# A graph network on 16 graphs: the next graph's sums and inverses move one layer earlier

## The chip, the cores and the metric

The kernel runs on one core of one Trainium2 chip. A core has a matrix engine (TensorE, PE in the profile, with its weight loads shown apart as PEld), three engines for vectors (VectorE or DVE, ScalarE or ACT, GpSimd or POOL) and SyncE (SP), which here issues nearly all DMA transfers. Each engine works through its own queue in order and waits on semaphores for the others. The metric is the device time of one execution in microseconds. The time before is 2472.18 us, the median of three runs (2469.78 to 2474.06).

## The reference

The inputs are `x`, 16 graphs of 1024 nodes with 128 features, and `adj`, a 1024 x 1024 matrix of weights for each graph, all in fp32.

```
# part 0
degree = adj.sum(axis=-1)[:, :, None]
nbr    = einsum('bid,bij->bjd', x, adj) / degree
x      = layernorm(x + relu(concat([x, nbr], -1) @ W.T + b))
# part 1: four layers on the same adj
src = nodes @ ws + bs;   src_agg = einsum('bjv,bij->biv', src, l2norm(adj, axis=2))
dst = nodes @ wd + bd;   dst_agg = einsum('bjv,bji->biv', dst, l2norm(adj, axis=1))
out = tanh(concat([src_agg, nodes @ wn + bn, dst_agg], 2) @ wu + bu)
```

The second and the later layers of part 1 get earlier outputs as well (inputs of 128, 128, 256 and 384 features). Its result gets a residual and a layer norm too. So each graph needs of its matrix: the sums of its rows (the degree), the sums of squares of its rows, and the sums of squares of its columns; the inverses of the first and the inverse roots of the others scale rows or columns.

## The kernel before

**Batches.** The kernel goes through the 16 graphs one after the other, here called batches 0 to 15. Its matrix `a` lies in SBUF as 128 partitions x 8 row blocks x 1024 columns. Two such buffers exist: while batch b is worked on, the matrix of batch b + 1 (`a2`, of index n in the code) is loaded, its sums are made, and part 0 of batch b + 1 is done. The first matrix has a start of its own.

**Layers.** Each layer l of part 1 first makes messages (`messages`, L605 and L608): the features times folded weights, in four groups of two row blocks, with half 1 of the nodes first (groups 2, 3, 0, 1); PE makes a group, DVE adds the bias. Then it aggregates (`aggregate`, L774) over the matrix scaled by columns (`a`) and over its transpose scaled by rows (`at`). The product is done by halves in the way of Strassen and Winograd, with seven products and sums of quarters of the matrices made by DVE: T2, T3, T4 from `a` and Q2, Q3, Q4 from `at` (`combine`, L587 to L591). Each step of the loop is a pair of matmuls on 64 columns of the array each, which run side by side. Layers zero and one have 30 steps, of which the first two are the layer's own weights; layer two has 32. M2 on Q2 begins at step 14 in layer one of batch 0, M3 on Q3 at step 18, Z21 on T4 at step 22 and on Q4 at step 26. Results of products are read between the steps: copies on ACT (L687, L688, L691, L692, L708), additions on DVE (L695, L712, L699, L703, L704) and at last L776; the tanh that ends each half is L787, and its output (f1T, f23T) is what the next layer's messages read.

**Hooks.** The order of the work on PE, DVE, ACT and POOL is written out by hand: what the program says first stands first in the queue of its engine. A dictionary of hooks gives, for a step of the aggregation, a function that is called ahead of that step's matmuls; `between` does so behind a group of the messages. A hook says only where its instructions stand in the queues. Its PE instructions do stand between two steps; DVE and ACT may come to theirs earlier or later. The order of DMA issues on SyncE is chosen by the framework.

**Sums of the next matrix.** ACT squares a row block (L253, with the row sum of squares as a by-product) into one of two buffers of tag `sq`, and sums a row block for the degree (`degree_of`, L248 on ACT, L246 on DVE). DVE adds the eight squares up, two buffers into `acc` first (L260) and then one after the other (L262). `column_sums` turns `acc` over in 32 x 32 pieces (L270) and reduces it to `part` (L275). `inverses` multiplies that by a constant (pc, L183 on PE), brings it to the right places (L299, L301, L306) and lets POOL raise all to the power -1/2 (L307). `inverse_rows` (L328 to L331) makes the inverse degree and writes all inverses to DRAM (`dr`, L333). `factor_row` reads a row of it back to all partitions (`cinv`, later `dinv`, L339). DVE scales the next matrix with `cinv` (L345, 16 instructions), then makes its quarters (L583, L452), the sums of x (`x_sums`, L441 to L445, on `xn` that `load_blocks` loads, L205), and `first_gnn` does part 0 of the next batch on PE: products at L516, sums T3 and T4 at L461 and L467, reads at L498 to L518, and last the weights (pw, L183), which read e1 (L508) and e0 (L518). It stands between layers two and three.

**Layer norm of the batch before.** In layer one its last norm is done: `begin1` (L354 to L361), `centre1` (pm on PE, L368, square L371 on ACT), `squares1` (L377), `rstd1` (pv on PE, L385, POOL L387); L392 and the stores of the output (L235) follow in layer two (`end1`).

**Buffers.** Tiles of one tag share a buffer, and the later one waits for the last reader of the earlier one. `acc` has tag "row", which `cinv` and `dinv` use as well; the intermediate sums of layer one have tag "acc".

Of the kernel before, what the change touches and what calls it, by code (L numbers as in the profile page):

```python
# [14 lines left out]
P = 128  # L15
# [8 lines left out]
def adj_resnorm_kernel(ctx: ExitStack, tc: tile.TileContext, x, adj, w0, b0, layers, out):  # L24
# [231 lines left out]
    def add_squares(b, state, i):  # L256

        if i == 1:
            state["acc"] = one.tile([P, N], F32, tag="row", name=f"acc{b}")
            nc.vector.tensor_add(state["acc"], state[0], state[1])  # L260
        elif i > 1:
            nc.vector.tensor_add(state["acc"], state["acc"], state[i])  # L262

    def column_sums(b, state):

        column_reduce(b, state, column_transpose(b, state))
# [69 lines left out]
    def factor_row(b, state, k, tag):  # L336
        r = one.tile([P, N], F32, tag="row", name=f"{tag}{b}")
        for h in range(NH):
            nc.sync.dma_start(r[:, half(h)].rearrange("p (g i) -> p g i", g=G),  # L339
                              state["dv"][k, h][None].to_broadcast([P, G, P]))  # L340
        return r
# [239 lines left out]
    def combine_1(y):  # L581

        nc.vector.tensor_sub(y[0, 1], y[0, 1], y[0, 0])  # L583

    def combine(i, y, T):
        if i == 2:
            nc.vector.tensor_sub(T[2], y[1, 1], y[0, 1])  # L587
        elif i == 3:
            nc.vector.tensor_sub(T[3], T[2], y[0, 0])
        else:  # L590
            nc.vector.tensor_sub(T[4], y[1, 0], T[2])  # L591
# [404 lines left out]
    for b in range(B):  # L996
# [8 lines left out]
        if b == 0:  # L1005
            def row_factors0():
                nonlocal rinv
                rinv = gather_inverses(0, row_inverses(0, inv))
                column_sums(0, st0)
                for q in (2, 3):  # L1010
                    scale_rows(rows[q], q, rinv)

            t = messages(b, 0, feats, wm, {0: lambda: to_x1(0), 2: row_factors0}, with_sums=False)
            cinv = {}

            def columns0(rows, h, engine=nc.vector):
                scale_columns(a, cinv[0], rows, half(h), engine)

            def rows0(destination, finish):
                for q in (2, 3):  # L1020
                    transpose_rows(rows[q], q, at)

            def cinv0(destination, finish):
                cinv[0] = factor_rows_now(0, 1, inv, "cinv")

            def second0(destination, finish):
                columns0(range(NJ, NB), 1)
                destination(1, cinv[0])
                columns0(range(NJ), 1)

            def fold_and_scale(l, q):
                fold_begin(l, fetched[l])
                scale_rows(rows[q], q, rinv)

            def first0(destination, finish):
                columns0(range(NJ, NB), 0, nc.gpsimd)
                columns0(range(2), 0, nc.gpsimd)
                for q in (0, 1):
                    transpose_rows(rows[q], q, at)
                destination(0, cinv[0])  # L1040
                columns0(range(2, NJ), 0)

            def sums0(destination, finish):
                combine_1(y)
                finish(1)
                combine(2, y, T)
                combine_1(yt)
                combine(3, y, T)

            def folded(l, part):  # L1050
                return lambda *_: part(l, fetched[l])

            hooks = {4: lambda *_: inverses(0, st0, NB), 5: folded(2, fold_begin), 6: rows0, 7: cinv0,
                     8: folded(2, fold_end), 9: lambda *_: fold_and_scale(3, 0), 11: second0, 12: folded(3, fold_end),
                     14: lambda *_: scale_rows(rows[1], 1, rinv), 18: first0, 26: sums0}
            T = combined(0, "T")
            plain_layer(b, 0, feats, t, a, at, f1, "acc", hooks)
            wm = message_weights(b, 1)
            a2 = load(n)
            xs2 = load_spread(n)  # L1060
        else:
            w = {}
            if nxt:
                w["a"] = load(n)
                st = begin_sums(n)
            t = messages(b, 0, feats, wm)
            wm = message_weights(b, 1)
            Q = combined(b, "Q")

            def rows3():  # L1070
                for q in (1, 0):
                    transpose_rows(rows[q], q, at)

            def sums1(w=w, st=st):
                if nxt:
                    for i in range(2):
                        squares_of_row(n, w["a"], st, i)
                    for i in range(2):
                        degree_of(w["a"], st, i)

            hooks = {0: rows3, 3: lambda: combine(4, y, T), 5: lambda: combine_1(yt), 7: lambda: combine(2, yt, Q),
                     9: lambda: combine(3, yt, Q), 11: lambda: combine(4, yt, Q),
                     17: sums1}
            aggregate(b, 0, feats, t, a, at, T, Q, f1, "row", hooks)
            a2, xs2 = w.get("a"), None

# [6 lines left out]
        def sums_of(*rows, of=(), engine=nc.scalar, add=()):  # L1093

            def issue():
                for i in of:
                    degree_of(a2, st, i, engine)
                for i in rows:
                    squares_of_row(n, a2, st, i)
                for i in add:  # L1100
                    add_squares(n, st, i)
            return issue

        hooks = {}
        if b == 0:
            def quarters2():
                for i in (2, 3, 4):
                    combine(i, yt, Q)

            hooks = {0: quarters2, 12: lambda: combine(4, y, T)}  # L1110
            st = begin_sums(n)
            hooks |= {5 + 2 * i if i < 3 else 4 + 3 * i: sums_of(i, of=(i,), engine=nc.scalar if i < BPH else nc.vector, add=(i,))
                      for i in ALL}
        else:
            nm = f"1_{b - 1}"
            w = {"ys": summed(f"y{nm}", "xa")}
            sums_of_next = {}
            if nxt:
                sums_of_next = {1: sums_of(2, 3, of=(2, 3), add=(2, 3)), 4: sums_of(of=(4, 5)), 10: sums_of(4, 5),
                                13: sums_of(add=(4, 5)), 16: sums_of(6), 17: sums_of(7),  # L1120
                                19: sums_of(of=(6,), add=(6,)), 22: sums_of(of=(7,), add=(7,)),
                                23: lambda: column_sums(n, st)}

            def begin1(w=w, nm=nm):
                if nxt:
                    add_squares(n, st, 1)
                norm_spread(w["ys"], f4, KS)
                w["s"] = norm_sum(w["ys"], KS, nm, back)

            def centre1(w=w, nm=nm):  # L1130
                w["sq"] = norm_centre(w["ys"], w["s"], KS, nm)
                if nxt:
                    w["xs"] = load_spread(n)

            def squares1(w=w, nm=nm):
                w["v"] = norm_squares(w["sq"], KS, nm)

            def rstd1(w=w, nm=nm):
                w["r"] = norm_rstd(w["v"], KS, nm)

            hooks = {0: begin1, 12: centre1, 14: squares1, 20: rstd1, **sums_of_next}
        aggregate(b, 1, feats, t, a, at, T, Q, f23, "acc", hooks)
        if b:
            second_norm, xs2 = w, w.get("xs")

# [11 lines left out]
        def start3(w=w):  # L1157
            w["xT"] = to_features(xs2, f"x{n}_")

        def sums3():  # L1160
            column_sums(n, st)

        def factors(w=w):
            w["xn"] = load_blocks(n)
            inverse_rows(n, st)
            w["cinv"] = factor_row(n, st, 1, "cinv")

        def factors_of_rows(w=w):
            w["spread"] = row_inverses(n, st["inv"])
# [18 lines left out]
        if nxt:  # L1188
            scales = [lambda: scale(0, 1), lambda: scale(NJ, 1), lambda: scale(0, 0), lambda: scale(NJ, 0)]
            if b == 0:  # L1190
                between = {1: sums3}
                hooks = {4: inverses3, 5: factors, 10: factors_of_rows, 11: start3, 18: factors_gathered,
                         **dict(zip((12, 15, 19, 25), scales))}
                quarters_at = (26, 27, 29)
            else:
                between = {0: inverses3, 1: end1, 2: factors}
                hooks = {0: factors_of_rows, 3: start3, **dict(zip((7, 9, 11, 13), scales)), 15: factors_gathered}
                quarters_at = (19, 21, 25)
            hooks |= dict(zip(quarters_at, (quarter1, x_sums, quarter2)))
        t = messages(b, 2, feats, wm, between)  # L1200
        wm = message_weights(b, 3)
# [154 lines left out]
```

## Time and profile before

| | |
|---|---|
| time | 2472.18 us (2469.78 to 2474.06) |
| span of the profiled execution, clock | 2471.2 us, 0.998 |
| busy: PE, DVE, ACT, POOL | 2444.3, 1913.8, 954.4, 273.6 us |
| batch 7: layer zero, messages, layer one, messages, layer two | 25.90, 3.65, 26.13, 7.54, 27.64 us |
| batch 7: aggregation for the next batch (L516), pw (L183) | 12.02, 4.00 us |
| batch 0: layer one, messages, layer two, then L516 and pw | 25.90, 12.99, 27.75, 22.01 us |

A line of the stretches reads: begin and end in us, length, then for PE, PEld, DVE, ACT and POOL the busy time with the number of instructions, the clock that TensorE was granted (1.00 is full), and the share and rate of the DMA engines. In a line of the timeline stand start, length, engine, line of the kernel, operation, what it writes and reads, shapes, and in brackets how long the engine was idle before it and what ended that. A line of the waits has who waited for whom, the total in us, how often, and the longest. The ends of matmuls are modelled, so PE counts as busy in most of its short waits; the distances between starts tell more.

### The profile page before, as it was taken

The numbers are of one execution on the slowest core, as the hardware profiler recorded it, in microseconds if no ns is written. First come the engines' busy times: TensorE is split into PE (matmuls) and PEld (weight loads), VectorE is DVE, ScalarE is ACT, GpSimd is POOL, SyncE is SP. The second block draws the span as 40 slices with busy tenths as digits, with TensorE's granted clock in tenths as the row PEclk, the third lists the DMA queues.
The fourth block names the chain that finished last, engine by engine and source line by source line (L and its number), as shares of the span: only waits on it lengthen the run. The fifth ranks groups of instructions, "written<-read, shape, count | busy, mean of one in ns | idle before, by whom it ended". The sixth has DMA issues, their size and how long they took to land. (4 is left out here: it accounts for less than half of the span.)

```text
span 2471.2 us, 30800 instructions
## 1 busy us (share of the span) xinstructions
PE 2444.3 (99%) x11453; PEld 1028.7 (42%) x11453; DVE 1913.8 (77%) x2499; ACT 954.4 (39%) x1786; POOL 273.6 (11%) x100
## 2 busy tenths in 40 slices
PE   8999999999999999999999999999999999999999
PEld 5443344433444334443444434334443344433444
DVE  5868878788787987778787787887878878798743
ACT  5315345153342534426243351534515334253321
POOL 4001111001111011110111100111101111101100
PEclk9999999999999999999999999999999999999999
DMA  9517244272542616335172452724426254261410
GB/s 206 101 40 151 58 96 94 59 141 52 115 90 62 132 43 137 75 78 108 44 162 51 89 103 54 145 58 94 95 60 141 52 116 92 58 132 43 95 24 9
DMA packets 365716, 219.68 MB, mean 89 GB/s; under 512 B 152768, under 2 KB 336832, under 8 KB 365568
## 3 DMA queue, kind: packets, MB, share of 16 engines
q1 hardware_dynamic: 364800, 215.36, 41.1%
q0 software_dynamic: 768, 2.36, 0.4%
q8 instruction: 91, 1.49, 0.3%
q14 instruction: 57, 0.47, 0.1%
HBM read 199.17 MB, written 18.46 MB: 88 GB/s over the span
## 5 line engine op out<-in xcount | busy, mean ns | idle before, releaser
L774 PE MATMUL m<-Q,S 128*64 128x512 f32 x1008 | 445.1, 593 | 1.3 <-DVE Q L587 1.3
L387 POOL TENSOR_TENSOR rs<-ve,mhalf 128x32 f32<-128x32 f32 x30 | 191.6, 6387 | 1975.1 <-DVE ve L385 1975.1
L774 PE MATMUL m<-T,S 128*64 128x512 f32 x1008 | 396.6, 593 | 0.0
L774 PE MATMUL m<-at,t 128*64 128x512 f32 x1008 | 394.4, 593 | 0.0
L774 PE MATMUL m<-a,t 128*64 128x512 f32 x1008 | 390.1, 593 | 0.0
L608 DVE TENSOR_TENSOR t<-pt,wm 128x512 f32<-128x512 f32 x256 | 176.5, 690 | 162.0 <-PE pt L605 160.0
L774 PEld LDWEIGHTS m<-Q,S 128*64 128x64 f32 x1008 | 136.2, 137 | 282.0 <-issue 269.8
L687 ACT COPY e<-m 64x512 f32<-64x512 f32 x63 | 36.7, 582 | 511.0 <-PE m L774 510.6
L774 PE MATMUL z<-a,S 128*64 128x512 f32 x504 | 228.3, 593 | 0.0
L774 PE MATMUL z<-a,t 128*64 128x512 f32 x504 | 226.8, 592 | 0.0
L774 PE MATMUL z<-at,S 128*64 128x512 f32 x504 | 226.7, 592 | 0.0
L774 PE MATMUL z<-at,t 128*64 128x512 f32 x504 | 226.6, 592 | 0.0
L774 PE MATMUL z<-Q,t 128*64 128x512 f32 x504 | 226.6, 592 | 0.0
L605 PE MATMUL pt<-wm,f1T 128*128 128x256 f32 x768 | 216.0, 387 | 0.1
L345 DVE TENSOR_TENSOR a<-a,cinv 128x512 f32<-128x512 f32 x250 | 154.3, 691 | 78.3 <-DMA cinv<-dr 77.0
L774 PEld LDWEIGHTS m<-at,t 128*64 128x64 f32 x1008 | 118.5, 137 | 143.9 <-issue 142.5
L774 PEld LDWEIGHTS m<-a,t 128*64 128x64 f32 x1008 | 120.1, 137 | 134.1 <-issue 121.3
L774 PE MATMUL z<-T,t 128*64 128x512 f32 x384 | 172.8, 592 | 0.0
L774 PEld LDWEIGHTS m<-T,S 128*64 128x64 f32 x1008 | 119.0, 137 | 127.3 <-issue 127.3
L605 PEld LDWEIGHTS pt<-wm,f1T 128*128 128x128 f32 x768 | 142.7, 190 | 44.4 <-issue 13.5
L605 PE MATMUL pt<-wm,f23T 128*128 128x256 f32 x512 | 153.4, 381 | 3.7 <-ACT f23T L787 3.7
L253 ACT ACTIVATE sq<-a 128x1024 f32<-128x1024 f32 x120 | 125.8, 1050 | 79.0 <-DVE acc L260 78.3
(239 smaller groups left out, 4281.4 us busy)
## 6 DMA issues: line engine op xcount, KB each, us to landing
a<-in_adj_dram SPq DMA_DIRECT2D x120, 512.0 KB, 11.0
a<-in_adj_dram SPq DMA_DIRECT2D x240, 128.0 KB, 4.2
rows<-in_adj_dram SPq DMA_DIRECT2D x240, 64.0 KB, 2.7
wm<-wsave SPq DMA_DIRECT2D x16, 512.0 KB, 4.1
xn<-in_x_dram SPq DMA_DIRECT2D x124, 64.0 KB, 1.9
wm<-wsave SPq DMA_DIRECT2D x31, 256.0 KB, 3.4
xs<-in_x_dram SPq DMA_DIRECT2D x60, 128.0 KB, 3.6
cinv<-dr SPq DMA_DIRECT2D x30, 256.0 KB, 5.5
```

The costliest lines, as they stand in the source:

```text
L253: nc.scalar.activation(sq, a[:, i, :], AF.Square, accum_out=state["cols"][:, i:i + 1])
L345: engine.tensor_mul(a[:, i, s], a[:, i, s], cinv[:, s])
L387: nc.gpsimd.tensor_tensor(rstd, ve, mhalf[:, :n], ALU.pow)
L605: nc.tensor.matmul(pt[:, q], f[:, i * P:(i + 1) * P], wm[:, 1 + c], start=(k == 0), stop=(k == nch - 1))
L608: nc.vector.tensor_add(t[j][:, o:o + 2].rearrange("p k a v c -> p k (a v c)"), pt, wm[:, 0][:, None, :].to_broadcast([P, 2, 2 * P]))
L687: nc.scalar.copy(e0[high], A[high])
L774: nc.tensor.matmul(o, x, y, start=start, stop=stop)
```

## The change

The change moves the sums of the next matrix, and what hangs on them, to earlier places. Its parts:

- In batches 1 to 15 the first addition of squares moves from layer one into layer zero (step 28). `acc` takes the tag "acc" and the sums of layer one take "row", so that `acc` can be written while layer zero still uses "row".
- In those batches the hooks of layer one are set anew, squares and row sums first, and `inverses` with its product pc moves from behind the second message group of layer two to step 29 of layer one. The norm's `centre1` and `rstd1` move one and two steps ahead.
- `factors` (inverses to DRAM and the row `cinv` back) follows the second message group, ahead of the norm's end and the loading of x, and the scaling of the matrix, its quarters and the sums of x take earlier hooks. The transpose of the next x (`start3`, L350) moves behind them.
- In batch 0 all row sums are done by ACT, the sums start with layer one and alternate with Q2, Q3, T4 and Q4, column sums move to step 27 of layer one, and `inverses` and `factors` into the messages of layer two.

```diff
@@ add_squares
-            state["acc"] = one.tile([P, N], F32, tag="row", name=f"acc{b}")
+            state["acc"] = one.tile([P, N], F32, tag="acc", name=f"acc{b}")
@@ layer zero, batches 1 to 15
+            def first_addition(st=st):
+                if nxt:
+                    add_squares(n, st, 1)
+
-                     17: sums1}
+                     ... 17: sums1, 28: first_addition}
@@ layer one, batch 0
-            def quarters2():
-                for i in (2, 3, 4):
-                    combine(i, yt, Q)
-
-            hooks = {0: quarters2, 12: lambda: combine(4, y, T)}
+            hooks = {0: sums_of(0, 1, add=(1,)), 1: lambda: combine(2, yt, Q), 2: sums_of(2, 3, add=(2, 3)),
+                     3: lambda: combine(3, yt, Q), 4: sums_of(4, 5, of=(0, 1), add=(4, 5)), 5: lambda: combine(4, y, T),
+                     11: sums_of(of=(2, 3)), 13: sums_of(6, 7, of=(4,)), 15: sums_of(of=(5,)),
+                     18: lambda: combine(4, yt, Q), 19: sums_of(of=(6, 7), add=(6, 7)), 27: lambda: column_sums(n, st)}
             st = begin_sums(n)
-            hooks |= {5 + 2 * i if i < 3 else 4 + 3 * i: sums_of(i, of=(i,), engine=nc.scalar if i < BPH else nc.vector, add=(i,))
-                      for i in ALL}
@@ layer one, batches 1 to 15
-                sums_of_next = {1: sums_of(2, 3, of=(2, 3), add=(2, 3)), 4: sums_of(of=(4, 5)), 10: sums_of(4, 5),
-                                13: sums_of(add=(4, 5)), 16: sums_of(6), 17: sums_of(7),
-                                19: sums_of(of=(6,), add=(6,)), 22: sums_of(of=(7,), add=(7,)),
-                                23: lambda: column_sums(n, st)}
+                sums_of_next = {1: sums_of(2, 3, add=(2,)), 2: sums_of(of=(2, 3, 4, 5)), 8: sums_of(4), 10: sums_of(add=(3,)),
+                                12: sums_of(5, add=(4,)), 15: sums_of(6, add=(5,)), 19: sums_of(7, add=(6,)),
+                                20: sums_of(of=(6,)), 21: sums_of(add=(7,)), 23: sums_of(of=(7,)),
+                                24: lambda: column_sums(n, st), 29: lambda: inverses(n, st)}
             def begin1(w=w, nm=nm):
-                if nxt:
-                    add_squares(n, st, 1)
-            hooks = {0: begin1, 12: centre1, 14: squares1, 20: rstd1, **sums_of_next}
-        aggregate(b, 1, feats, t, a, at, T, Q, f23, "acc", hooks)
+            hooks = {0: begin1, 11: centre1, 14: squares1, 18: rstd1, **sums_of_next}
+        aggregate(b, 1, feats, t, a, at, T, Q, f23, "row", hooks)
@@ layer two
-        def sums3():
-            column_sums(n, st)
-
         def factors(w=w):
-            w["xn"] = load_blocks(n)
             inverse_rows(n, st)
             w["cinv"] = factor_row(n, st, 1, "cinv")
+
+        def load_xn(w=w):
+            w["xn"] = load_blocks(n)
+
+        def end1_and_load():
+            load_xn()
+            end1()
             if b == 0:
-                between = {1: sums3}
-                hooks = {4: inverses3, 5: factors, 10: factors_of_rows, 11: start3, 18: factors_gathered,
-                         **dict(zip((12, 15, 19, 25), scales))}
-                quarters_at = (26, 27, 29)
+                between = {1: inverses3, 3: factors}
+                hooks = {1: load_xn, 5: factors_of_rows, 7: start3, 18: factors_gathered,
+                         **dict(zip((10, 12, 14, 16), scales))}
+                quarters_at = (20, 22, 25)
             else:
-                between = {0: inverses3, 1: end1, 2: factors}
-                hooks = {0: factors_of_rows, 3: start3, **dict(zip((7, 9, 11, 13), scales)), 15: factors_gathered}
-                quarters_at = (19, 21, 25)
+                between = {0: factors, 1: end1_and_load}
+                hooks = {2: factors_of_rows, **dict(zip((4, 5, 7, 9), scales)), 10: factors_gathered, 16: start3}
+                quarters_at = (12, 14, 25)
```

In the diff, `sums_of(rows, of=, add=)` squares the row blocks `rows`, sums those of `of` for the degree and adds the squares of `add`; `quarters_at` gives the hooks of the first quarter, the sums of x and the second quarter.

More of the change, by code (lines that the diff above doesn't have):

```diff
@@ L1079, in sums1 @@
                         degree_of(w["a"], st, i)
+            def first_addition(st=st):
+                if nxt:
+                    add_squares(n, st, 1)
             hooks = {0: rows3, 3: lambda: combine(4, y, T), 5: lambda: combine_1(yt), 7: lambda: combine(2, yt, Q),
-                     9: lambda: combine(3, yt, Q), 11: lambda: combine(4, yt, Q),
-                     17: sums1}
+                     9: lambda: combine(3, yt, Q), 11: lambda: combine(4, yt, Q), 17: sums1, 28: first_addition}
             aggregate(b, 0, feats, t, a, at, T, Q, f1, "row", hooks)
```

## The prediction

> **What bounds the kernel now.** I read the page first, then who TensorE (PE) waited for, then stretches of the trace by stage, then the queues of VectorE (DVE), ScalarE (ACT), GpSimd (POOL) and the DMA issuer SyncE around each gap. The page says that PE has work for 99% of the span, so time can come only out of PE's own gaps.
>
> ```profile
> PE 2444.3 (99%) x11453; PEld 1028.7 (42%) x11453; DVE 1913.8 (77%) x2499; ACT 954.4 (39%) x1786; POOL 273.6 (11%) x100
> ```
>
> The waits of PE between 84 and 176 us, batch 0's layers one and two, name the only two long gaps after the start:
>
> ```profile
> PE m_f L516 <- DVE xn L443: 3.7, 1, 3.7
> PE pt L605 <- ACT f23T L787: 3.7, 2, 2.2
> ```
>
> Four stretches of batch 0 (layer one; messages of layer two; layer two; the aggregation for batch 1, L516 and L183) beside the last batch's messages, where nothing is late:
>
> ```profile
> 84.86:110.76 25.90, 25.90 (x121) 8.55 (x121) 22.82 (x21) 12.76 (x25) 0.00 (x0) 1.00 0.32 50
> 110.76:123.75 12.99, 9.33 (x35) 7.01 (x33) 10.63 (x12) 4.02 (x7) 0.00 (x0) 0.87 0.09 27
> 123.75:151.50 27.75, 27.75 (x137) 9.47 (x137) 17.57 (x34) 4.85 (x8) 2.90 (x1) 1.00 0.16 46
> 151.50:173.51 22.01, 18.28 (x74) 6.69 (x71) 18.75 (x29) 5.54 (x9) 0.00 (x0) 0.92 0.09 25
> ...
> 2387.40:2394.50 7.10, 7.10 (x34) 5.99 (x32) 2.76 (x4) 0.72 (x1) 0.00 (x0) 1.00 0.00 0
> ```
>
> The messages take 12.99 us against 7.10: 5.9 us lost. The last stretch takes 22.01 us against 12.02 + 4.00 in batch 7: 6.0 us lost. In both the granted clock falls to 0.5 after the wait (the 0.87 and 0.92).
>
> Later batches lose little but often. After the aggregation for the next batch, PE multiplies its result by the weights (pw, L183) and waits for DVE:
>
> ```profile
> 1228.30 1.03 PE L183 MATMUL pw<-e_f,w0T 128*64 128x512 f32 x4
> 1229.58 1.08 PE L183 MATMUL pw<-e_f,w0T 128*64 128x512 f32 x4 [0.25 <-DVE e_f L518]
> ```
>
> and over the 14 pw stretches of batches 1 to 14 together (4.19 us each; the sum of the stretches first, then busy times):
>
> ```profile
> sum 58.72, PE 54.40 PEld 12.37 DVE 38.42 ACT 13.21 POOL 0.00; mean PE 3.89 PEld 0.88 DVE 2.74 ACT 0.94 POOL 0.00
> ```
>
> Matmuls start there 0.43 us apart when nothing waits, so eight starts and 0.1 us to the next stage need 3.53 us; 58.7 - 14 x 3.53 = 9.3 us are waits. In batch 7 DVE reaches that point late because its scaling of the next matrix started late:
>
> ```profile
> 1197.05 9.72 DVE L345 TENSOR_TENSOR a<-a,cinv 128x512 f32<-128x512 f32 x16 [4.97 <-DMA cinv<-dr]
> ...
> 1228.83 0.69 DVE L518 TENSOR_TENSOR e_f<-e_f,dinv 128x512 f32<-128x512 f32 x1
> ```
>
> [...] ACT stands 8.22 us before one square while row sums behind it are ready. [...] in batch 0 dr is issued at 131.94 and cinv at 133.42. [...]
>
> **The change, part by part.**
>
> *Column sums and inverses of the next matrix, batches 1 to 14.* The first addition moves into layer zero (step 28). DVE ends L704 there at 1148.48 and starts L776 at 1149.73, so 1.22 us fit in idle time: cost nothing. That frees both square buffers 8 us earlier, so ACT squares rows 2 and 3 at 1151 and not at 1158; all its sums still lie beside PE work.
>
> The product pc then stands in PE's queue ahead of step 29 of layer one and not behind the second message group. Times are from the layer's start, 1153.26. Steps are 0.8586 apart, two small products add 0.23, so step 29 comes at 25.2. DVE's chain to pc's operand: M2 ends at step 18, L695 can start at 15.85; with the starts that the trace has between such instructions L712 follows after 1.37, then 0.72, 0.22, 1.27, 1.14, 0.72, 0.79, 0.61 and 1.28 (L385, two additions, L699, L703, L704, L270, L275), and L275 takes 1.22. It ends at 25.2: PE waits about 0.1 us, or 0 to 0.4. ACT is not in the way (square of row 6 ends at 16.1, its copy L696 is wanted at 16.55). For this pc leaves a place where it costs 7.54 - 7.10 = 0.44 us (it splits a run of 256-column matmuls) for one where a like product, rp, shifts the row by 0.12. Per batch -0.44 + 0.12 + 0.12 = -0.20: **-2.8 us** over 14, with ends of -4.5 and +1.
>
> *Factor rows.* POOL's power (2.90 us) now starts at about 26.3, not 29.5, and DVE has invt at 30, 1183.3 in batch 7. dr no longer stands behind the four stores of the output (issued from 1185.44), so it goes at 1183.3 and not 1188.21; with batch 0's 1.5 us to cinv and 5.5 to the first scaling (133.42 to 138.89), and up to 1 us for the stores now beside it, scaling starts at 1191 to 1192, not 1197.05. The transpose of x (1.25 us) moves behind it. DVE then has everything before L695 done by 1204.9, when PE delivers, instead of 1209.10, and from there follows PE: L776 1214.8 (was 1217.54), L498 1221.75 (was 1223.06). Z0 is ready at 1226.85, so L517 and L518 end at 1228.35; PE wants that at 1229.1. The waits of pw go: **-9.3 us** of 14 batches, at worst -5 if some lateness stays.
>
> *Batch 0, layer one.* Row sums leave DVE (four of 1.2 us), and Q2, Q3 and T4 alternate with additions. DVE: addition 88.54, Q2 to 92.0 (wanted at step 14, 97), Q3 to 96.6 (100.4), T4 to 101.2 (103.9). ACT from 89.8, when the first addition frees the buffers: four squares and two row sums at 1.09 to 96.4, three copies to 98.2, three row sums and two squares to 103.6, two copies to 104.7, a row sum to 105.8, then L696. This is a new wait: L712 needs L696 and stands at the head of DVE from 101.9 to 106.5, with Q4 behind it; Q4 ends at 109.5 and PE wants it at step 26, 107.2. PE stops about 2.2 us (0.5 to 3) and ends the layer at 113.0, not 110.76. DVE goes on with two additions, L699, L703, L704 (to 114.0), tanh to 114.8: PE waits 1.4 us for f23T where it waited 1.47. The column sums end at 116.4, L776 at 117.0, tanh at 117.8, before PE wants it at 118.8, so the wait of 2.19 and the slow clock behind it go. pc costs 0.44 here. Layer two starts at 122.1 against 123.75: **-1.7 us**, between -4 (ACT quicker) and +1 (half clock after the new stop, 1.7 us, partly inside the next wait).
>
> *Batch 0, layer two.* inverses follows group two: POOL 119.6 to 122.5, dr at 123.5 beside the weights' DMA, cinv at about 126.5, scaling at 132 and not 138.89. Sixteen at 0.61 end at 141.8; quarter one, x's sums (1.7) and L695 to L704 bring DVE to 149.6 and quarter two to 152.6. The aggregation for batch 1 starts at 149.75 and wants T2 at 153.2, T3 at 156.6, T4 at 158.3; L461 ends at 155.7, L467 at 158.3. The wait of 3.73 us and the slow clock go: 17.67 becomes 12.02, **-5.7 us**, and pw loses another **-0.4**.
>
> Nothing else changes what PE waits for: the waits for Q2 in layer zero (L587, 2.6 us together) stay. Sum: -2.8 - 9.3 - 1.7 - 5.7 - 0.4 = -19.9, or 2452.3; I say **2453**.
>
> **Rivals.** *Only batch 0 gains:* the stores delay cinv, or L518 stays late for another cause, and pc's new wait eats what its place saves. For it: the pw waits vary from 0.2 to 1.3 us between like batches, which my chain doesn't explain. Against: all of DVE's lateness in batch 7 is accounted for. 2472.2 - 7.8 = 2464.4. *More than I sum:* ACT runs ahead in batch 0, Q4 comes in time, pc never waits: -1.7 more for pc and -2.3 more in layer one, 2448.5. *Slower:* pc now stands ahead of matmuls that are ready, so any lateness of the last addition is paid by PE. Were ACT one square and one row sum late (2.2 us) in all 14 batches, +31, less the 9.3 and 7.8 that stay: 2486. For it: no slack on DVE. Against: ACT has half a microsecond to spare, and its total work is unchanged.
>
> **How the numbers follow.** Forecast 0.67, only batch 0 0.13, more 0.14, slower 0.06 with smaller lateness in it. The range holds the forecast with its bounds and the better case, and reaches to the first rival without going far beyond: 2447 to 2464. Faster by over 0.2% (4.9 us) 0.94: the first three. Within 0.2% 0.03 and slower 0.03 share the last.
>
> **What would show it.** Right: in the stretches of batch 0 the messages of layer two near 9 us with one wait near 1.4 us on f23T; a wait of m or z on Q (L591) near 107 us in layer one; no wait on xn L443, clock 1.00 after 125 us; pw stretches near 3.5 us; messages of layer two at 7.1 us in batches 1 to 14 and layer one at 26.2 to 26.4; first scaling 5 us earlier. Wrong: pw waits unchanged, or PE waits on part L275 of over 0.4 us each.

## The result, and the profile after

The changed kernel takes 2456.17 us (2455.62 to 2456.82), the kernel before 2470.98 us beside it (2468.33 to 2474.06): a ratio of 0.994, 95% interval 0.9922 to 0.9957. It is faster by 14.8 us, where 19.2 were forecast; the predicted time of 2453.0 is 3.2 us short, and the measured one lies within the range. The profiled spans are 2471.2 and 2454.6 us, 16.6 apart: the execution of the kernel before that was profiled took 2472.99 us, 2.0 over the median.

The page after, PE's busy time, which was 2444.3:

```profile
PE 2433.6 (99%) x11453; PEld 1026.5 (42%) x11453; DVE 1909.8 (78%) x2495; ACT 956.8 (39%) x1794; POOL 287.2 (12%) x100
```

Whom PE waited for in batch 0's layers one and two (the same 84 to 176 us as before):

```profile
PE z L774 <- DVE Q L591: 1.9, 1, 1.9
PE pt L605 <- ACT f23T L787: 1.1, 1, 1.1
PE pw L183 <- DVE e_f L518: 0.3, 1, 0.3
```

The wait of 3.7 us on xn L443 is gone and the one on f23T is cut from 3.7 to 1.1; a new one on Q4 stands in layer one. The same four stretches as before (layer one; messages of layer two; layer two; L516 and L183):

```profile
84.69:112.67 27.98, 26.12 (x121) 8.46 (x120) 23.20 (x21) 19.00 (x37) 0.00 (x0) 1.00 0.26 42
112.67:121.58 8.91, 7.81 (x38) 6.03 (x37) 6.32 (x11) 1.57 (x3) 2.40 (x1) 1.00 0.21 57
121.58:149.21 27.63, 27.63 (x133) 9.36 (x134) 21.46 (x37) 3.97 (x7) 0.51 (x1) 1.00 0.21 58
149.21:165.55 16.34, 15.99 (x74) 4.88 (x70) 14.20 (x23) 6.42 (x11) 0.00 (x0) 1.00 0.00 1
```

Layer one costs 2.1 us more, its neighbour 4.1 less, the last stretch 5.7 less, and the clock is 1.00 in all four, where it was 0.87 and 0.92 in two.

The 14 pw stretches of batches 1 to 14, summed as before:

```profile
sum 49.42, PE 49.42 PEld 14.08 DVE 25.23 ACT 9.64 POOL 0.00; mean PE 3.53 PEld 1.01 DVE 1.80 ACT 0.69 POOL 0.00
```

They took 58.72; now each takes the 3.53 us of a stretch without a wait. Where the time went, as distances between the starts of the stages on PE (without the rounding of the stretches above):

| stage | before | after | difference |
|---|---|---|---|
| batch 0: layer one | 25.90 | 27.98 | +2.1 |
| batch 0: messages, layer two | 40.74 | 36.54 | -4.2 |
| batch 0: L516 | 17.67 | 12.02 | -5.65 |
| batch 0: pw | 4.35 | 4.32 | 0.0 |
| batches 1 to 14: layer zero | 365.17 | 365.27 | +0.1 |
| layer one | 365.88 | 372.49 | +6.6 |
| messages of layer two | 105.56 | 99.46 | -6.1 |
| layer two and L516 | 555.11 | 555.11 | 0.0 |
| pw | 58.72 | 49.47 | -9.3 |

The sum is -16.4, the whole difference of the spans but for 0.2, by which the start ahead of layer one was shorter. Two rows nearly cancel: what the messages gain by losing pc, layer one gives back.

### The profile page after: what moved, and what is told of

It reads as the page before. It is cut to its first block, busy times and chain, and to the rows that moved or that the text cites. A ratio compares the mean times of both kernels' runs of the same rounds, so it can differ in the third digit from the quotient of the medians.

```text
span 2454.6 us, 30806 instructions
## 1 busy us (share of the span) xinstructions
PE 2433.6 (99%) x11453; PEld 1026.5 (42%) x11453; DVE 1909.8 (78%) x2495; ACT 956.8 (39%) x1794; POOL 287.2 (12%) x100
## 4 chain that ended last, share of the span: by engine, by line
PE 84%; DVE 6%; DMA 5%; SPq 1%; ACT 1%; issue 1%; DVEq 0%; POOLq 0%; ACTq 0%
PE m L774 37%; PE z L774 21%; PE pt L605 15%; PE m_f L516 5%; DMA a<-in_adj_dram 3%; PE pw L183 2%; PE z_f L516 2%; SPq L549 1%; DVE at L564 1%; DMA rows<-in_adj_dram 1%; DVE acc L262 1%; DMA rows_acc<-in_adj_dram 1%; DMA raw<-in_L_gnn_ws_dram 1%; DVE at L583 1%; DVE Q L587 0%
## 5 line engine op out<-in xcount | busy, mean ns | idle before, releaser
L387 POOL TENSOR_TENSOR rs<-ve,mhalf 128x32 f32<-128x32 f32 x30 | 205.2, 6840 | 1972.2 <-DVE ve L385 1972.2
## 6 DMA issues: line engine op xcount, KB each, us to landing
a<-in_adj_dram SPq DMA_DIRECT2D x120, 512.0 KB, 10.8
```

Source lines behind the costliest of these rows:

```text
L387: nc.gpsimd.tensor_tensor(rstd, ve, mhalf[:, :n], ALU.pow)
```

## The experiments

My theory: the gain has two separate sources, pw and batch 0's long waits; pc's early place is worth nothing, because PE waits 0.3 us for `part` each time. Rivals: that pc's small products cost 0.4 us wherever they stand, without any wait; that the earlier hooks on DVE, not the earlier request for `cinv`, free pw; that batch 0's early sums are what holds PE up later. The changed kernel was not run beside each: on the three chips used, the kernel before took 2471.2, 2474.4 and 2475.8 us, so differences of a microsecond or two between medians say little, and the stages of the traces decide.

### Is it a wait that eats pc's gain?

The timeline of the changed kernel around pc in batch 7, first PE, then the weight loads, then DVE's last step:

```profile
1165.78 0.59 PE L774 MATMUL z<-a,t 128*64 128x512 f32 x1
1166.51 0.31 PE L183 MATMUL pc<-part,fold 128*64 128x32 f32 x4
1166.62 0.62 PE L774 MATMUL z<-Q,t 128*64 128x512 f32 x1
...
1166.48 0.23 PEld L183 LDWEIGHTS pc<-part,fold 128*64 128x64 f32 x4 [0.98 <-issue]
...
1165.14 1.22 DVE L275 TENSOR_REDUCE part<-acct 128x32 f32<-128x1024 f32 x1
```

Pairs of matmuls start 0.43 us apart, so pc could start at 1166.21. `part` is ready at 1166.36 and pc starts at 1166.51: 0.30 late. Layer one is as long (26.60 or 26.61 us) in all 14 batches. The list of waits doesn't show it, since the modelled end of the matmul before (1165.78 + 0.59 = 1166.37) covers most of it; only the distance between starts does.

**Sums ahead of the reads.** In layer one the last addition and the column sums stand ahead of L699, L703 and L704; pc stays at step 29.

```diff
+            def last_sums(st=st):
+                add_squares(n, st, 7)
+                column_sums(n, st)
-   20: sums_of(of=(6,)), 21: sums_of(add=(7,)), 23: sums_of(of=(7,)), 24: lambda: column_sums(n, st), 29: ...
+   20: sums_of(of=(6,)), 21: last_sums, 23: sums_of(of=(7,)), 29: ...
```

> The changed kernel with the column sums of batches 1 to 14 ahead of the reads L699 to L704 on DVE, so that part is ready 2.5 us earlier, and pc where the change puts it. Theory (pc waits because DVE's chain from L695 ends 0.2 us after PE comes to step 29): no wait on part, layer one at 26.25 us, the tanh that ends half 1 at 26.2, still ahead of the first message; time 2456.2 - 14 x 0.36 = 2451. Rival (the 0.30 us are a cost of the switch itself, not of the wait): unchanged, 2456. Rival (the tanh comes too late and PE waits for f23T): over 2457.

Measured: 2451.68 us (2451.12 to 2452.64), ratio to before 0.9921 (0.9907 to 0.9936), 4.5 under the changed kernel. Its PE, weight loads and DVE at the same place:

```profile
1163.71 0.59 PE L774 MATMUL z<-a,t 128*64 128x512 f32 x1
1164.13 0.26 PE L183 MATMUL pc<-part,fold 128*64 128x32 f32 x4
1164.22 0.62 PE L774 MATMUL z<-Q,t 128*64 128x512 f32 x1
...
1163.70 0.14 PEld L183 LDWEIGHTS pc<-part,fold 128*64 128x64 f32 x2 [0.28 <-issue]
...
1160.96 1.22 DVE L275 TENSOR_REDUCE part<-acct 128x32 f32<-128x1024 f32 x1
```

`part` is ready at 1162.18, two microseconds ahead; pc follows its forerunner by 0.42, and layer one is 26.25 us long against 26.61, and against 26.13 without pc. So pc itself costs 0.12 here and the wait 0.36 of the layer. The rival of small products that are dear everywhere falls.

**pc at the border of the stages.** `inverses` stands between layer one's last step and the first message of layer two.

```diff
-   24: lambda: column_sums(n, st), 29: lambda: inverses(n, st)}
+   24: lambda: column_sums(n, st)}
...
+        if b and nxt:
+            inverses(n, st)
         t = messages(b, 2, feats, wm, between)
```

> The changed kernel with pc between layer one's last matmul and the first message of layer two, not ahead of step 29, in batches 1 to 14. Theory (pc's wait of 0.30 us for part is the only thing lost there): layer one at 26.13 us and not 26.61, pc costs 0.15 to 0.25 us at the border of the stages, messages of layer two start unwaited; time 2456.2 - 14 x 0.2 to 0.35 = 2451 to 2453.5. Rival (any product of 32 columns next to the messages costs the 0.44 us it cost among them): 2455.5 to 2456.5.

Measured: 2451.22 us (2450.57 to 2451.92), 0.9919 (0.9904 to 0.9934), 4.9 under the changed kernel. Layer one takes 26.22, messages 7.10: pc costs 0.09 here, and 0.86 us of later place is enough for `part`.

**pc back in its old place**, with the factor rows behind the third group and the rest of the change kept.

```diff
-   24: lambda: column_sums(n, st), 29: lambda: inverses(n, st)}
+   24: lambda: column_sums(n, st)}
-                between = {0: factors, 1: end1_and_load}
+                between = {0: inverses3, 1: factors, 2: end1_and_load}
```

> The changed kernel with pc back among the messages of layer two (behind the first group) in batches 1 to 14, and the factor rows behind the second group. Theory (the early place of pc gives nothing by itself: 0.44 us less among the messages, 0.47 more in layer one; the row of factors comes 1.7 us later, and DVE has the slack): layer one 26.13 us, messages 7.54, pw 3.53 to 3.6; time 2455.7 to 2456.5. Rival (the early place is what brings the scaling ahead of PE): pw at 3.8 or more, time over 2460.

Measured: 2456.12 us (2454.98 to 2456.93), 0.9924 (0.9908 to 0.9941): the time of the changed kernel. Layer one 26.13, messages 7.54, pw 3.53 in all 14. `dr` is issued 3 us later than in the changed kernel, but still ahead of the stores, and scaling begins 2.7 us later (batch 7). As changed, the move of pc brings nothing, neither by its own cost nor by making `cinv` earlier.

### What frees pw: the request or the hooks?

In batch 7 of the changed kernel SyncE issues dr and cinv 3.5 and 2 us ahead of layer two's start (1174.74), and ahead of the stores. The timeline of SyncE and of DVE:

```profile
1171.25 0.34 SPq L333 DMA_DIRECT2D dr<-invt  x1
1172.77 0.94 SPq L339 DMA_DIRECT2D cinv<-dr  x2
1173.80 5.53 SPq L235 DMA_DIRECT2D out_dram<-y  x4
...
1178.92 9.72 DVE L345 TENSOR_TENSOR a<-a,cinv 128x512 f32<-128x512 f32 x16 [0.31 <-DMA out_dram<-y]
...
1214.39 1.89 PE L183 MATMUL pw<-x_T,w0T 128*64 128x512 f32 x8
1216.11 1.89 PE L183 MATMUL pw<-e_f,w0T 128*64 128x512 f32 x8
```

Scaling starts 4.2 us into layer two, 10.1 before. DVE waits 0.3 us ahead of it, where it waited 5.0.

**Factor rows late**, in batches 1 to 14, hooks as changed:

```diff
-                between = {0: factors, 1: end1_and_load}
+                between = {1: end1_and_load, 3: factors}
```

> The changed kernel with the factor rows asked for behind the last message group of layer two in batches 1 to 14, so that the stores of the output go ahead of them again, as before the change; early product pc and all other hooks as changed. Theory (the start of the scaling sets whether pw waits): first scaling about 5 us later, DVE late at L518 again, pw at 4.1 to 4.4 us and not 3.53; time 2456.2 + 14 x 0.6 to 0.9 = 2465 to 2469. Rival (the new order of DVE's work in layer two, with x's transpose behind the scaling and the quarters earlier, removed the wait): pw stays at 3.53 us, time 2456 to 2457. Rival (pc's early place did it): the same 2456 to 2457.

Measured: 2485.11 us (2483.01 to 2487.55), ratio 1.006 (1.0043 to 1.0076): slower than before, and some 18 us over what I expected. Its waits of PE, and DVE in batch 7 (layer two from 1186.07):

```profile
PE pw L183 <- DVE e_f L508: 11.7, 15, 0.9
PE pw L183 <- DVE e_f L518: 4.1, 15, 0.3
PE m_f L516 <- ACT e_f L493: 2.1, 4, 0.7
```

```profile
1190.16 0.18 DVE L312 TENSOR_TENSOR sp<-inv,group 128x32 f32<-128x32 f32 x1
1196.82 9.72 DVE L345 TENSOR_TENSOR a<-a,cinv 128x512 f32<-128x512 f32 x16 [6.47 <-DMA cinv<-dr]
...
1210.47 1.24 DVE L350 STREAM_TRANSPOSE x_T<-xs 128x1024 f32<-128x1024 f32 x1
1211.74 0.69 DVE L695 TENSOR_TENSOR e<-e,m 64x512 f32<-64x512 f32 x1
```

DVE stands 6.5 us with nothing else to do, and x's transpose, which used to fill part of that wait, comes after it. `dr` is again issued behind the stores, 1.4 us into layer two (1.3 before). pw takes 5.06 us a batch, against 4.19 before, and L516 12.36 against 12.02. I had expected about the old state; I hadn't counted that the new hooks need the early request.

**The old hooks of layer two**, with the request early, and with it late:

```diff
-   hooks = {2: factors_of_rows, **dict(zip((4, 5, 7, 9), scales)), 10: factors_gathered, 16: start3}
-   quarters_at = (12, 14, 25)
+   hooks = {0: factors_of_rows, 3: start3, **dict(zip((7, 9, 11, 13), scales)), 15: factors_gathered}
+   quarters_at = (19, 21, 25)
```

> The changed kernel with the hooks of layer two of batches 1 to 14 as before the change (x's transpose ahead of the scaling, quarter one behind step 19), but the factor rows asked for early, as changed. With the run that asks late this makes a table of two by two. Theory (the early request alone removes the wait): first scaling about 5 us into layer two, pw 3.53 us, time 2456 to 2456.5. Rival (request and order are both needed): pw 3.7 to 4.1, time 2459 to 2464.

> The changed kernel with both the late request and the old hooks of layer two in batches 1 to 14, so that only pc's early place and layer one are left of the change there. Theory: first scaling 10 us into layer two as before, pw near 4.2 us as before; time 2456.2 + 14 x 0.66 = 2465. Of the 29 us that the late request cost with the new hooks, 20 then belong to the new order, in which x's transpose (1.25 us) no longer lies in the wait for the factor rows. Rival (the late request is worse by itself because of the DMA traffic beside it): pw near 5 us, time over 2475.

Measured: early 2457.25 us (2456.05 to 2458.4), 0.9927 (0.9911 to 0.9944), pw 3.53 in batches 1 to 14; late 2469.75 us (2466.3 to 2471.64), 0.9979 (0.9971 to 0.9986), pw 4.53 on average. The late one is 5 us over my figure: `dr` is issued as late as before, but in batch 7 cinv lands 0.7 us later, and scaling begins 10.8 us into layer two. DVE of the early one, layer two from 1175.91:

```profile
1183.80 1.25 DVE L350 STREAM_TRANSPOSE x_T<-xs 128x1024 f32<-128x1024 f32 x1 [4.03 <-DMA out_dram<-y]
1184.97 9.68 DVE L345 TENSOR_TENSOR a<-a,cinv 128x512 f32<-128x512 f32 x16
```

Here the transpose stands first and waits for the stores: `x_T` takes over the buffer of `y` (tag "xa"), whose last store landed at 1183.62. cinv was there at 1180.61. Scaling begins 9.1 us into layer two, only 1 us earlier than before the change, and still no pw waits. Batch 7 in six kernels: when scaling begins and when DVE starts the first read of the aggregation (L498), both from layer two's start, and pw:

| request, hooks | scaling | L498 | pw |
|---|---|---|---|
| early, new (changed) | 4.18 | 34.76 | 3.53 |
| early, new, pc in its old place | 6.90 | 34.76 | 3.53 |
| early, old | 9.07 | 35.06 | 3.53 |
| before | 10.11 | 36.13 | 4.00 |
| late, old | 10.78 | 36.80 | 4.67 |
| late, new | 10.75 | 37.89 | 5.14 |

So the request frees pw; the new hooks with a late request make it worse, and with the early request they add slack that nothing uses.

How late DVE was can be read from the kernel before, whose 14 pw stretches differ. Its fastest and its slowest, batches 5 and 13 (layer two from 885.70 and from 2093.01):

```profile
895.55 9.72 DVE L345 TENSOR_TENSOR a<-a,cinv 128x512 f32<-128x512 f32 x16 [4.74 <-DMA cinv<-dr]
2103.91 9.72 DVE L345 TENSOR_TENSOR a<-a,cinv 128x512 f32<-128x512 f32 x16 [5.78 <-DMA cinv<-dr]
...
925.35:929.09 3.74, 3.74 (x18) 0.94 (x14) 2.58 (x4) 0.69 (x1) 0.00 (x0) 1.00 0.02 4
2132.66:2137.46 4.80, 3.98 (x19) 0.86 (x15) 2.95 (x5) 1.30 (x2) 0.00 (x0) 1.00 0.00 0
```

Scaling begins 9.85 and 10.90 us into layer two, and pw takes 3.74 and 4.80. In all 14 batches scaling begins 0.02 us after the last piece of cinv has landed, and pw takes the time from layer two's start to that landing, less 6.08, to within 0.01 us. Its two reads of 256 KB are issued from 3.9 to 5.3 us into layer two and take 5.4 to 6.9 us to this landing; each tenth by which they land later goes straight into PE's wait. Without a wait pw takes 3.53, so cinv had to land by 9.61 and came 0.2 to 1.3 us later: that much was missing, not the 5.9 us by which the change moves the scaling in batch 7.

### Batch 0

**Batch 0 as before**, the later batches as changed (its hooks of layers one and two, and `between`, as in the lines with a minus in the change):

```diff
-            hooks = {0: sums_of(0, 1, add=(1,)), 1: lambda: combine(2, yt, Q), 2: sums_of(2, 3, add=(2, 3)), ...
+            hooks = {0: quarters2, 12: lambda: combine(4, y, T)}
...
-                between = {1: inverses3, 3: factors}
+                between = {1: lambda: column_sums(n, st)}
```

> The changed kernel with batch 0's hooks of layers one and two as they were before; the other batches keep the change. Theory (batch 0 gives 7.8 us, the later batches 8.8): messages of layer two of batch 0 back at 12.99 us, the first aggregation for the next batch at 17.67, the clock halved twice, pw of batches 1 to 14 still 3.53 us each; time 2456.2 + 7.8 = 2464. Rival (the gain is all in the later batches, batch 0's new stop of 1.9 us gives back what it saves): 2456 to 2458. Rival (the parts depend on each other: a late batch 0 makes the next ones late): over 2466.

Measured: 2463.06 us (2461.47 to 2464.88), 0.9968 (0.9955 to 0.9981), 6.9 over the changed kernel; the waits on xn (4.0) and f23T (3.7) are back, and other batches keep pw at 3.53. Two of its stretches, messages of layer two, and L516 with pw:

```profile
110.53:121.83 11.30, 7.64 (x34) 5.83 (x33) 10.46 (x12) 4.02 (x7) 0.00 (x0) 1.00 0.11 30
...
149.58:171.90 22.32, 18.28 (x74) 6.68 (x71) 19.06 (x30) 5.82 (x10) 0.00 (x0) 0.92 0.09 25
```

The messages take 11.30 us here and took 12.99 in the kernel before, with the same waits (1.47 and 2.19 us): the clock didn't fall this time (1.00 for 0.87). So 1.7 us of the gain between the traces of before and after belongs to the clock, and layer one with these messages gains only 0.3 us over this run (37.20 to 36.89). How often the clock falls here in other executions is not shown.

**Q4 ahead.** The timeline of DVE shows what the new stop in layer one of the changed kernel is:

```profile
101.15 0.69 DVE L695 TENSOR_TENSOR e<-e,m 64x512 f32<-64x512 f32 x1
106.04 0.69 DVE L712 TENSOR_TENSOR e<-e,e 64x512 f32<-64x512 f32 x1 [4.19 <-ACT e L696]
106.74 2.29 DVE L591 TENSOR_TENSOR Q<-at,Q 128x2048 f32<-128x2048 f32 x1
```

DVE is idle for 4.19 us with Q4 behind the waiting L712. In the next kernel Q4 comes ahead of L695; in the one after that, additions 6 and 7 as well:

```diff
-   11: sums_of(of=(2, 3)), 13: ...      18: lambda: combine(4, yt, Q), 19: sums_of(of=(6, 7), add=(6, 7)), ...
+   7: lambda: combine(4, yt, Q), 11: sums_of(of=(2, 3)), 13: ...      19: sums_of(of=(6, 7), add=(6, 7)), ...
# and in the second kernel also
-   19: sums_of(of=(6, 7), add=(6, 7))
+   17: sums_of(add=(6, 7)), 19: sums_of(of=(6, 7))
```

> The changed kernel with Q4 of batch 0's layer one made on DVE right behind T4, ahead of L695 and L712. Theory (PE stops 1.9 us at step 26 only because Q4 stands behind L712, which waits for ACT): the wait on Q L591 goes, layer one of batch 0 at 25.9 us and not 27.98, and part of it comes back as a longer wait for f23T, since DVE has its reads no earlier than 2.2 us before; messages of layer two at 9.3 to 9.6 us; time 2456.2 - 1.5 = 2454.7. Rival (DVE's total work up to the end of the layer decides): layer and messages together stay at 36.9 us, 2456.2.

> As the run with Q4 ahead, and the last two additions of squares in batch 0 ahead of L695 as well, in the time in which DVE waits for ACT. Theory: neither Q L591 nor f23T is waited for in batch 0; layer one 25.9 us, messages of layer two 7.54, together 3.4 us less than in the changed kernel: 2452.8. Rival (L696 on ACT then comes later, and f23T with it): messages still 8.5 or more, over 2453.8.

Measured: Q4 alone 2455.05 us (2454.39 to 2455.84), 0.9919 (0.9904 to 0.9934); layer one is back at 25.90, the messages take 8.79, 2.2 us less together. The span got only 0.6 us shorter, since the start ahead of layer one, which the edit doesn't touch, took 1.8 us longer in this trace. With the additions 2453.73 us (2452.66 to 2455.51), 0.9914 (0.99 to 0.9929), 2.4 under the changed kernel where 3.4 were expected. Its messages, and the last stretch:

```profile
110.10:118.17 8.07, 7.81 (x39) 6.03 (x37) 5.58 (x10) 1.44 (x2) 2.40 (x1) 1.00 0.01 3
...
145.80:162.65 16.85, 16.00 (x75) 4.88 (x71) 14.70 (x23) 6.88 (x11) 0.00 (x0) 1.00 0.00 0
```

0.3 us of the wait on f23T stays, and the last stretch has grown by 0.5: pw now waits 0.6 us for L508, since PE reaches it earlier and DVE doesn't.

### All of it together

The second of those batch 0 kernels, with the sums ahead of the reads:

> The changed kernel with both remedies: batch 0's Q4 and last additions ahead of L695, and the column sums of batches 1 to 14 ahead of the reads. Theory: the two parts add, 2456.2 - 3.4 - 5.0 = 2447.8. Rival (one of the two gives nothing): 2451 to 2453.

Measured: 2448.1 us (2447.79 to 2449.71), 0.9892 (0.9878 to 0.9907), 8.1 under the changed kernel and faster than both. The gains add up: 2.4 + 4.5 = 6.9 from the single runs; by the stages 14 x 0.36 = 5.0 in layer one and 2.7 in batch 0, 7.7. Layer one of the later batches 26.25, batch 0's layer one 25.90 and messages 8.08.

## Why the prediction was right, and where it was off

**pc and the inverses, -2.8: measured +0.5.** This is the term that was mis-sized, by 3.3 us. Between the traces the change gives -16.6 where the terms had summed to -19.9; the other errors cancel. Of "-0.44 + 0.12 + 0.12 = -0.20", the -0.44 (messages 7.54 to 7.10) and the first 0.12 (26.13 to 26.25 without a wait) came out. The wait was to be 0.12 and measured 0.36 in the length of the layer, 0.30 between the starts. Half of that is DVE: L695 began 15.82 into the layer as predicted (15.85), but the two additions and the start of L699 took 2.59 and not 1.27 + 1.14, so `part` came at 25.33 and not 25.2. The other half is the step from L275's end to pc's start (1166.36 to 1166.51), which the prediction counted as nothing. The stated end of +1 held it.

**Factor rows, -9.3: measured -9.3.** In batch 7, from layer one's start, dr was predicted at 30.0 and issued at 30.2, scaling at 37.7 to 38.7 and begun at 37.9, L776 at 61.5 and begun at 61.6, L498 at 68.5 and begun at 68.5. L695 came 1.2 us late (52.8 for 51.6), which 2.0 us of idle time ahead of L776 took up. The mechanism holds, but the prediction didn't ask how much of the 5 us pw needed: 0.2 to 1.3 us would have done. Nor was moving the transpose of x needed for pw, as the early request with the old hooks shows.

**Batch 0, layer one, -1.7: measured -2.0** (+2.1 - 4.1). That the sum fits is in part luck: 1.7 us of it is the half clock (3.41 us at 0.50) in the one trace of the kernel before, which the prediction took as given, and beside a trace without it 0.3 us is left. The new wait is the one described: L712 idle from 101.84 to 106.04 (101.9 to 106.5 predicted), Q4 done at 109.03 (109.5), PE's stop 1.9 (2.2), the wait on f23T 1.1 (1.4). The half clock named for the bad end did not come.

**Batch 0, layer two, -5.7: measured -5.65**, L516 at its 12.02. **pw of batch 0, -0.4: measured 0.0**: it takes 4.35 and 4.32 us, 0.8 over a stretch without waits in both, since the end of L516 moved forward with everything else.

**The rivals.** With only batch 0 gaining the pw stretches would have stayed at 58.7. The better case needed Q4 in time and no wait of pc: those are just the two edits that, with two additions moved, give 2448.1, where 2448.5 had been worked out (its terms sum to 2448.3). For pc the better case said -4.5, and layer one with the messages gives that (+1.6 - 6.1). The slower one needed late additions; they were late by tenths.

The prediction left unexplained why like batches had pw waits between 0.2 and 1.3 us, and counted this for its first rival. The trace it was made from answers it: the waits follow the landing of cinv. Why the same two reads take 1.5 us longer in one batch than in another is not shown. Without these waits the times lie closer (2455.6 to 2456.8, against 2468.3 to 2474.1); that the landings make that spread fits, but only one execution was traced.

## What to carry to other kernels

An instruction placed early in the queue of the engine that bounds the kernel saves its cost only if its operand is there before its turn (among the messages pc cost 0.44 us, in layer one 0.12 and a wait of 0.36): count the step behind the last producer (0.15 us here), and leave some tenths of slack, or place it at the next border of stages, where here it cost 0.09 us and waited for nothing. Look for such waits in distances between starts, since the modelled ends hid most of this one of 0.30 us. When a late engine makes the bound one wait, find out how much of its lateness counts: here at most 1.3 of the 5.9 us by which scaling moved paid, and the new order of the work behind it without the early request made the kernel slower than before (ratio 1.006). Where like stretches differ, line up their lengths with the landing of the DMA that releases them: here that gave the missing time to a hundredth.

## What the runs showed of the hardware

- For pc the first weight load stood 0.43 us ahead of its matmul where `part` was ready (1163.70 and 1164.13, with the sums ahead of the reads), and 0.03 us where PE waited (1166.48 and 1166.51, in the changed kernel), though what it loads is the constant `fold` and not `part`. So where PE waited, the pair waited together; which of the two held the wait is not shown. From the end of `part` to the load it took 0.12 us.
- The four products of pc (128x32) cost 0.44 us between matmuls of 256 columns of the messages (7.54 against 7.10), 0.12 between steps of the aggregation (26.25 against 26.13) and 0.09 at the border between the two (26.22).
- The two reads that bring a row of `dr` to all partitions (256 KB each) took 5.4 to 6.9 us from the first issue to the last landing in 14 like batches of the kernel before.
- In the profile of the kernel before, the granted clock was 0.50 for 3.41 us after the stop of 2.2 us (119.48 to 122.89; messages 12.99 us) and for 3.41 us after the stop of 3.7 us (157.03 to 160.44). In the profile with batch 0 as before, the stops of 1.5 and 2.2 us were the same and the clock stayed at 1.00 (messages 11.30), while it was 0.92 over the stretch with the stop of 4.0 us; it stayed at 1.00 after the new stop of 1.9 us in the changed kernel too. What decides whether the clock falls is not shown.
